# The gated adapter matrix of the second batch: from TensorE in batch 1's attention to ScalarE and GpSimd in batch 0's feed-forward half

## The chip, the cores and the metric

The kernel runs on one core of a Trainium2 chip, with every engine of that core: TensorE (PE; its weight loads, PEld, overlap its matmuls), VectorE (DVE), ScalarE (ACT), GpSimd (POOL) and SyncE (SP, which only issues DMAs). The metric is the device time of one execution in microseconds (us), as a median over runs. The kernel before takes 1123.19 us, the median of 3 runs from 1122.52 to 1124.55 us.

## The reference, cut to what matters

`x` is (2, 1024, 2048), `ctx` (2, 2048, 2048), the feed-forward weight `kernel` 2048 x 2048, all f32. There are 8 groups of 256 tokens (four to a batch), 16 adapters of rank 32, and a shared adapter.

```python
x = x + matmul(fake_quant(layernorm(x)), fake_quant(ctx))   # quantised cross attention
h = layernorm(x)
base   = matmul(h, kernel) + bias
A_eff  = einsum('bn,nri->bri', gate, lora_A)   # (8,16) x (16,32,2048): gated A of each group
B_eff  = einsum('bn,nor->bor', gate, lora_B)   # gated B
Ax     = einsum('bri,bti->btr', A_eff, h.reshape(8, 256, 2048))
delta  = einsum('bor,btr->bto', B_eff, Ax)
delta += einsum('or,btr->bto', lora_B_shared, einsum('ri,bti->btr', lora_A_shared, h))
x = x + base + delta
```

`A_eff` and `B_eff` are called the gated A and the gated B below. The change concerns only how the gated A of the second batch's four groups is made.

## The kernel before, in words

**Stages.** One loop runs over the two batches. Each turn has an attention stage and a feed-forward half (`ffn`). In the trace the product stage of the first feed-forward half lies at about 243 to 545 us; batch 1's attention starts inside its end and runs to about 790 us; the second feed-forward half follows.

**Attention.** The context comes in four blocks of 512 columns. Each block is loaded in eight tiles of 512 KB from `todo`, a list set out by hand at L155 to L164, which `load_next` (L170) works off in order on SP's queue, up to nine tiles ahead of use, each into a buffer of `lit` (ten buffers of 4 KB a partition). `quantise` (L310) rounds a tile to integers (ScalarE at L314 into one of the three `q2b` buffers, VectorE at L317 back out in bf16), `column_term` adds the zero-point term of the block, and `xattn_pair` (L350) multiplies one group's layernormed, quantised tokens by a block on TensorE (`pa`, L361) and adds it to `y`, the residual in SBUF. It also leaves layernorm sums in `st2`.

**The gated matrices.** `gated` (L376) makes one 128 x 512 piece of a gated matrix on TensorE: all 512 rows (16 adapters by 32) of a block of 512 columns stand in two `lit` tiles, loaded by four DMAs of 256 KB; four fp32 matmuls with `gmat`, the gates laid out as a matrix, sum over the adapters (L383); VectorE copies the PSUM result to a `q2b` buffer (L395). For A, `lora_a_step` (L398) then transposes the piece in four 128 x 128 parts on TensorE (L403) and VectorE copies them with four instructions to `acat` (L406), which holds A with the input dimension on the partitions: `acat[p, k, column, r]`, where the columns 0, 2, 3 and 5 belong to the four groups and 1 and 4 to the shared A. There are four such steps in a batch: two while block 2 is quantised (after its tiles 3 and 7) and two between the pairs of block 2. For B, `lora_b_step` (L411) stores the pieces to a DRAM tile `bd`.

**Between attention and feed-forward.** `prep_z` (L422) normalises a tile of 128 tokens with VectorE (L257 to L261 give its mean and deviation; `sd_z` at L261 is ScalarE's), transposes it on TensorE in packs of four (`ptz`, L432, two PSUM buffers, as `ps_m` has) and copies each pack out with ScalarE (L433). `group_z` (L435) stores each group's `z` to DRAM (`zs`) on ScalarE's DMA queue. `lora_ax` (L442) multiplies `acat` with z for two groups (`px`, L448), and ScalarE copies the result to `axT`.

**Feed-forward.** The 1024 x 2048 by 2048 x 2048 product is made by Strassen's scheme on two levels: 7 outer products (index `o`) of 7 inner products each (index `s`). `product` (L607) is one of these 49: 8 fp32 matmuls, which the trace records as 16 of 128 x 512, in PSUM chains named fu, fv and fw (L619), 6.87 us a product. `spread` adds a finished chain to the blocks of `y` with VectorE (L637). The operands are sums of blocks, built ahead by `Operands`: the left ones (names a and s) in `lit` buffers, loaded from `zs` and combined on GpSimd; the right ones (b and t) in `big` buffers, loaded from the weight and combined on VectorE; L559 is `block`, L568 is `comb`. The tables `BEGIN`, `BLOCKS`, `AHEAD`, `OWN` and `DROP` say behind which inner product each is loaded, combined and given back. `Delta.step` (L470) runs in inner products 1 and 4 of outer products 0 to 3: it loads a piece of the gated B and of the bias (`bp`, `bias`) on ScalarE's DMA queue, copies the bias into PSUM with ScalarE (L480, L483), multiplies by `axT` (`pl`, L491) and adds to `y` with VectorE (L502). There are eight such steps in a feed-forward half. The last outer product of batch 0 also starts batch 1's attention (`meanwhile`: block 0 is quantised and the first `prep_x` run).

**Order.** A scheduler places the instructions on each engine by their dependences and the program's order. `line` (L507) overrides it on VectorE alone: each of the feed-forward's VectorE additions is made to follow the one before it in the program. GpSimd's are placed by the scheduler.

**Layout that the change reaches.** `st1` and `st2` (L124, L125) are the layernorm sums of the attention input and output, each 128 x 8 x 4 x 6. `gate_b` is the gate on every partition, (8, 16); it is masked in place with `m_ad` at the program's start to make `gval`, from which `gmat` is filled for each batch. After the attention's block 2 in batch 0, the shared A is loaded to `acat` by SP (L750) and the shared B to `bd` (L753).

Of the kernel before, what the change touches and what calls it, by code (L numbers as in the profile page):

```python
# [10 lines left out]
F32 = mybir.dt.float32  # L11
# [4 lines left out]
ALU = mybir.AluOpType  # L16
# [4 lines left out]
P = 128  # L21
# [45 lines left out]
def tile_quant_xattn_then_lora_ffn(  # L67
# [32 lines left out]
    KQ = KT // 4  # L100
    GP = GPB * RC

    const = ctx.enter_context(tc.tile_pool(name="const", bufs=1))
# [4 lines left out]
    ps_m = ctx.enter_context(tc.tile_pool(name="ps_m", bufs=2, space=PSUM))  # L108
# [6 lines left out]
    q2b = Bufs([const.tile([P, 2, NB], I16, tag=f"q2b{i}", name=f"q2b{i}") for i in range(3)])  # L115

    acat = const.tile([P, KT, GPB // 2 * 3, R], F32, tag="acat", name="acat")
    own_col = [0, 2, 3, 5]
# [2 lines left out]
    bias_b = Bufs([const.tile([P, NB], F32, tag=f"bias{i}", name=f"bias{i}") for i in range(1)])  # L121
    axT = const.tile([P, GPB // 2, GT], F32, tag="axT", name="axT")
    gmat = const.tile([P, 2, GPB // 2, RC], F32, tag="gmat", name="gmat")
    st1 = const.tile([P, MT, NN, 6], F32, tag="st1", name="st1")  # L124
    st2 = const.tile([P, MT, NN, 6], F32, tag="st2", name="st2")  # L125
    r_s = const.tile([P, MT], F32, tag="r_s", name="r_s")

    zs = [
# [11 lines left out]
    def flat(t):  # L140
        return t.rearrange("p k n -> p (k n)")
# [14 lines left out]
    for b in range(B):  # L156
        for n in range(2):
            todo.extend((b, raw_src(b, n, r)) for r in range(KT // 2))
        for n in range(2, 4):
            for r in range(KT // 2):  # L160
                todo.append((b, raw_src(b, n, r)))
                if r in ((3, 7) if n == 2 else (5, 7)):
                    todo.extend((b, ad_src(la, 2 * (n - 2) + r // 6 if n == 3 else r // 4, h)) for h in range(2))
        for n in range(NN):  # L164
            todo.extend((b, ad_src(lb, n, h)) for h in range(2))
# [51 lines left out]
    ident = const.tile([P, P], F32, tag="ident", name="ident")  # L217
# [11 lines left out]
    for tag in ("acc0", "acc1", "delta"):  # L229
# [212 lines left out]
    def lora_ax(b, pr, zqs):  # L442
# [12 lines left out]
                )  # L455
        nc.scalar.copy(axT[:, pr, :], px)

    class Delta:


        def __init__(self, b):
            self.b = b


            self.banks = [ps_m.tile([P, NB], F32, tag="pm", name=f"pl_{b}_1{i}") for i in range(2)]
            for t in self.banks:
                nc.tensor.matmul(t, ones_h, ones_h[:, 0:1].to_broadcast([P, NB]), start=True, stop=True)
            self.units = deque((pr, n) for pr, n in ((0, 2), (0, 3), (0, 0), (0, 1), (1, 0), (1, 1), (1, 2), (1, 3)))
# [37 lines left out]

    def line(ins):  # L507

        if ins.ins.engine == mybir.EngineType.DVE:
            if line.last is not None:  # L510
                tc.add_manual_dep(
                    ins.ins,
                    line.last.name,
                    mybir.DependencyInfo(mybir.DependencyClass.NoSync, mybir.DependencyReason.DATA),
                    reason="line",
                )
            line.last = ins.ins

    line.last = None

    NO = len(OUTER)
    last_use = {}
# [4 lines left out]
    class Operands:  # L527
# [7 lines left out]
        def load(self, name):  # L535

            i, j = int(name[1]) - 1, int(name[2]) - 1
            a_terms, b_terms, _ = OUTER[self.o]
            got = []
            if name[0] == "a":  # L540
                for I, K, _ in a_terms:
                    t = lit.take()
                    nc.sync.dma_start(out=t, in_=zs[self.b][2 * I + i][2 * K + j])
                    got.append(t)
            else:
                for K, J, _ in b_terms:
                    t = big.take()
                    k0, n0 = (2 * K + i) * KQ * P, (2 * J + j) * NB
                    nc.sync.dma_start(out=t, in_=w[ds(k0, KQ * P), ds(n0, NB)].rearrange("(k p) n -> p k n", p=P))
                    got.append(t)  # L550
            self.wait[name] = got
# [91 lines left out]
    def ffn(b, ops, meanwhile):  # L643

        delta = Delta(b)
        for o in range(NO):
            nxt = Operands(b, o + 1) if o + 1 < NO else None
            chains = {}
            for s in range(len(INNER)):
                product(b, o, s, ops, chains)  # L650
                if s in OWN:
                    OWN[s](ops)
                if nxt and s in AHEAD:
                    AHEAD[s](nxt)
                spread(b, o, s, chains)
                if s in (1, 4):
                    delta.step()
                added = line.last
                if nxt:
                    for name in BLOCKS.get(s, ()):  # L660
                        nxt.block(name)
                for name in DROP.get(s, ()):
                    ops.drop(name)
                if nxt:
                    for name in BEGIN.get(s, ()):
                        nxt.load(name)
                with tc.issue_after(added):
                    meanwhile(o, s)
            ops = nxt
# [31 lines left out]
    for b in range(B):  # L701
# [30 lines left out]
        for g in range(2, GPB):  # L732
            for m in range(g * MG, (g + 1) * MG):
                with tc.issue_after(opened.ins):
                    prep_x(b, m, c1T, wk)
            for n in range(2):
                xattn_pair(b, n, g, c1T, c2[n])
                if g + 1 == GPB:
                    close_c2(n)
                    open_c2(n + 2)  # L740
                    bp.give(colt.pop(n))
                    if n == 0:
                        for r in range(NR):
                            quantise(c2[2], r)
                            if r % 4 == 3:
                                lora_a_step(b, r // 4)
                        column_term(b, 2, c2[2])
        if b == 0:
            for pr in range(GPB // 2):
                nc.sync.dma_start(out=acat[:, :, 3 * pr + 1, :], in_=a_sh)  # L750
            for bb in range(B):
                for g in range(GPB):
                    nc.sync.dma_start(out=bd[bb][g, 1 - g % 2], in_=b_sh)  # L753
        for g in range(GPB):
            xattn_pair(b, 2, g, c1T, c2[2])
            for r in {0: range(3), 1: range(3, 6), 2: range(6, 8), 3: ()}[g]:
                quantise(c2[3], r)
            if 1 <= g <= 2:
                lora_a_step(b, g + 1)
            if g == 2:  # L760
                column_term(b, 3, c2[3])
# [156 lines left out]
```

## Time and profile before

The profile is of one execution, which took 1122.67 us; the span from its first to its last instruction is 1120.9 us. It is 0.5 us under the median of the runs.

| | from the profile before |
|---|---|
| profiled execution, span | 1122.67 us, 1120.9 us |
| median of 3 runs (lowest to highest) | 1123.19 us (1122.52 to 1124.55) |
| matmuls of the feed-forward products, fu, fv and fw at L619 | 395.3 + 198.1 + 99.2 = 692.6 us, 593 ns each |
| attention matmuls, `pa` at L361 | 233.3 us, 381 ns each |
| GpSimd's 128 x 1024 operations, L559 and L568 | 99.8 + 160.3 us, 2497 and 2872 ns each |
| VectorE's 128 x 2048 operations, L559 and L568 | 102.2 + 161.5 us, 2554 and 2888 ns each |
| ScalarE's share of the span | 23% (261.6 us), most of it in the attention stages |
| DMA | 261.35 MB, 233 GB/s on average |
| of it adapter A (`lit<-in_lora_a_dram`) | 32 DMAs of 256 KB, SP's queue |

A row of the profile's groups names the line and engine, the operation, the tile written and the tiles read, partitions by elements, the count, then the busy time of the group in us with the mean of one in ns, and last the idle time of the engine before them and what ended most of it. The chain of waits is followed back from the last instruction, and gives 82% of its length to TensorE. The order of the rows of a timeline or a chain is that of time: start, length, engine, line, operation.

### The profile page before, as it was taken

The numbers are of one execution on the slowest core, as the hardware profiler recorded it, in microseconds if no ns is written. First come the engines' busy times: TensorE is split into PE (matmuls) and PEld (weight loads), VectorE is DVE, ScalarE is ACT, GpSimd is POOL, SyncE is SP. The second block draws the span as 40 slices with busy tenths as digits, with TensorE's granted clock in tenths as the row PEclk, the third lists the DMA queues.
The fourth block names the chain that finished last, engine by engine and source line by source line (L and its number), as shares of the span: only waits on it lengthen the run. The fifth ranks groups of instructions, "written<-read, shape, count | busy, mean of one in ns | idle before, by whom it ended". The sixth has DMA issues, their size and how long they took to land.

```text
span 1120.9 us, 10622 instructions
## 1 busy us (share of the span) xinstructions
PE 1066.2 (95%) x3898; PEld 493.9 (44%) x3930; DVE 745.5 (67%) x969; ACT 261.6 (23%) x358; POOL 260.7 (23%) x106
## 2 busy tenths in 40 slices
PE   1689999999999999999999999999999999999998
PEld 0344334554444444444444433455444444444443
DVE  4685547565697767668777654766568686865851
ACT  5875513220000000001375761232100000000000
POOL 0000000223353421534000000021534343253600
PEclk6799999999999999999999999999999999999999
DMA  8991946786789757499867095488768875749511
GB/s 307 393 248 36 281 127 233 265 319 234 246 283 374 281 175 261 153 328 322 286 187 226 1 280 151 180 301 313 253 225 293 302 260 175 260 145 322 208 38 56
DMA packets 120772, 261.35 MB, mean 233 GB/s; under 512 B 11920, under 2 KB 16144, under 8 KB 119568
## 3 DMA queue, kind: packets, MB, share of 16 engines
q1 hardware_dynamic: 99264, 218.65, 57.0%
q10 hardware_dynamic: 21456, 42.02, 11.0%
q8 instruction: 31, 0.51, 0.2%
q14 instruction: 21, 0.17, 0.0%
HBM read 224.99 MB, written 37.75 MB: 234 GB/s over the span
## 4 chain that ended last, share of the span: by engine, by line
PE 82%; DMA 7%; DVE 4%; ACT 4%; issue 1%; SPq 1%; ACTq 0%; DVEq 0%
PE fu L619 33%; PE fv L619 17%; PE pa L361 12%; PE fw L619 9%; DMA lit<-in_ctx_dram 4%; PE pl L491 3%; PE ptz L432 2%; DMA bd<-q2b 2%; DMA zs<-lit 1%; PE px L448 1%; PE pg_a L383 1%; DVE st L283 1%; PE pg_b L383 1%; ACT big L298 1%; ACT big L295 1%
## 5 line engine op out<-in xcount | busy, mean ns | idle before, releaser
L619 PE MATMUL fu<-big,lit 128*128 128x512 f32 x896 | 395.3, 593 | 0.0
L568 POOL TENSOR_TENSOR lit<-lit,lit 128x1024 f32<-128x1024 f32 x56 | 160.3, 2872 | 529.1 <-DMA zs<-lit 403.1
L619 PEld LDWEIGHTS fu<-big,lit 128*128 128x128 f32 x896 | 168.7, 190 | 206.2 <-issue 205.2
L361 PE MATMUL pa<-big,big 128*128 128x512 bf16 x992 | 233.3, 381 | 13.1 <-ACT pa L359 9.5
L619 PE MATMUL fv<-big,lit 128*128 128x512 f32 x448 | 198.1, 594 | 0.0
L559 POOL TENSOR_TENSOR lit<-lit,lit 128x1024 f32<-128x1024 f32 x40 | 99.8, 2497 | 293.6 <-DMA lit<-zs 261.9
L568 DVE TENSOR_TENSOR big<-big,big 128x2048 f32<-128x2048 f32 x56 | 161.5, 2888 | 5.7 <-PE ptz L432 5.1
L361 PEld LDWEIGHTS <-big 128*128 128x128 bf16 x1024 | 97.0, 98 | 144.5 <-issue 42.3
L637 DVE TENSOR_TENSOR y<-y,fu 128x1024 f32<-128x1024 f32 (+1 forms) x98 | 113.7, 1194 | 63.6 <-PE fu L619 63.3
L619 PEld LDWEIGHTS fv<-big,lit 128*128 128x128 f32 x448 | 84.3, 190 | 105.0 <-issue 104.7
L637 DVE TENSOR_TENSOR y<-y,fv 128x1024 f32<-128x1024 f32 x48 | 56.8, 1218 | 88.3 <-PE fv L619 88.3
L314 ACT ACTIVATE q2b<-lit,sc,inv 128x1024 int16<-128x1024 f32 x64 | 76.6, 1230 | 156.8 <-DMA lit<-in_ctx_dram 137.2
L559 DVE TENSOR_TENSOR big<-big,big 128x2048 f32<-128x2048 f32 x40 | 102.2, 2554 | 11.1 <-DMA big<-in_w_dram 11.1
L619 PE MATMUL fw<-big,lit 128*128 128x512 f32 x224 | 99.2, 592 | 0.0
L370 DVE SCALAR_TENSOR_TENSOR y<-pa,k_s,y 128x1024 f32<-128x1024 f32 x32 | 41.0, 1282 | 69.6 <-PE pa L361 69.6
L480 ACT COPY pl<-bias 128x1024 f32<-128x1024 f32 x16 | 16.3, 1018 | 293.9 <-DVE y L502 280.9
L359 ACT ACTIVATE pa<-bp,r_s 128x512 f32<-128x512 f32 x64 | 42.8, 683 | 105.4 <-PE pa L361 60.2
L619 PEld LDWEIGHTS fw<-big,lit 128*128 128x128 f32 x224 | 42.2, 190 | 51.8 <-issue 51.6
L637 DVE TENSOR_TENSOR y<-y,fw 128x1024 f32<-128x1024 f32 x24 | 28.4, 1217 | 50.5 <-PE fw L619 50.5
L303 PE MATMUL pt<-ident_h,big 128*128 128x128 bf16 x256 | 20.3, 231 | 29.7 <-ACT big L298 29.4
L283 DVE BATCH_NORM_STATS2 st<-y 128x6 f32<-128x512 f32 x64 | 42.0, 676 | 2.7 <-DMA y<-in_x_dram 2.7
L317 DVE TENSOR_SCALAR big<-q2b 128x1024 bf16<-128x1024 int16 x64 | 27.5, 439 | 22.6 <-ACT q2b L314 19.4
(82 smaller groups left out, 630.5 us busy)
## 6 DMA issues: line engine op xcount, KB each, us to landing
big<-in_w_dram SPq DMA_DIRECT2D x96, 1024.0 KB
lit<-zs SPq DMA_DIRECT2D x88, 512.0 KB
lit<-in_ctx_dram SPq DMA_DIRECT2D x64, 512.0 KB
out_dram<-y ACTq DMA_DIRECT2D x30, 512.0 KB
zs<-lit ACTq DMA_DIRECT2D x24, 512.0 KB
y<-in_x_dram SPq DMA_DIRECT2D x8, 1024.0 KB
lit<-in_lora_a_dram SPq DMA_DIRECT2D x32, 256.0 KB
lit<-in_lora_bt_dram SPq DMA_DIRECT2D x32, 256.0 KB
```

Of the source, the lines that this page charges most:

```text
L283: nc.vector.bn_stats(st1[:, m, n, :], ym[:, ds(n * NB, NB)])
L314: nc.scalar.activation(qi, t, AF.Relu, bias=z2, scale=inv2)
L317: nc.vector.tensor_scalar(c2[r // 4][:, ds(2 * (r % 4), 2), :], qi, QMAX, CENTRE, ALU.min, ALU.subtract)
L359: nc.scalar.activation(pa[:, j, :], colt[n], AF.Identity, bias=r_s[:, m : m + 1])
L361: nc.tensor.matmul(pa[:, j, :], c1T[g][:, k, ds(j * P, P)], c2[k // 8][:, k % 8, :], start=False, stop=(k == KT - 1), skip_group_check=True,)
L370: summed = nc.vector.scalar_tensor_tensor(yp, pa, s12, yp, ALU.mult, ALU.add)
L383: nc.tensor.matmul(ps[row : row + GP, :], gmat.rearrange("p i a r -> p (i a r)"), t[:, c, :], start=True, stop=True, skip_group_check=True,)
L491: nc.tensor.matmul(pl[j][i][:, half], axT[rows, pr, ds(j * P, P)], bt[rows, half], start=False, stop=True, skip_group_check=True,)
L559: line(eng.tensor_tensor(got[0], got[0], got[1], ALU.add if terms[1][2] > 0 else ALU.subtract))
L568: line(eng.tensor_tensor(out_t, at[p], at[q], op))
L619: nc.tensor.matmul(ps[:, m, :], at[:, k, ds(m * P, P)], bt[:, k, :], start=(opens and k == 0), stop=(ends and k == KQ - 1), skip_group_che ...
L637: line(nc.vector.tensor_tensor(yp, yp, chains[chain][:, js, :], ALU.add if sign > 0 else ALU.subtract))
```

## The change

**Batch 1's gated A is no longer made in its attention.** In `todo`, the adapter A tiles are listed for batch 0 only, and the four calls of `lora_a_step` are made for batch 0 only. The gated B stays as it was.

**A new class `Gates` makes it in the feed-forward half of batch 0.** An adapter is 32 x 2048 numbers; it is loaded as a tile of 128 partitions by 512 (partition = 4 r + quarter of the columns) by one DMA of 256 KB from GpSimd's queue. For each of the four groups ScalarE multiplies it by that group's gate for the adapter, a number per partition from `gate_b`, and GpSimd adds the product into `acat`'s columns of the group; the first adapter is multiplied straight into `acat`. So there are 64 ScalarE multiplies, 60 GpSimd additions and 16 loads. When an adapter is done, the next one's load is issued. `SLOTS` names the 16 places (outer and inner product) behind which one adapter each is done: outer products 0 to 5. In inner products 5 and 6 of outer product 5, `turn` brings each group's 128 x 512 sum into the layout of `acat`: ScalarE copies it to a buffer, TensorE transposes it in four parts (`pgt`, in the `ps_m` buffers), ScalarE copies the result to `acat`. Two groups are turned in each of the two places.

**Buffers.** The ring of four 128 x 512 buffers is made of the three `q2b` buffers, which the feed-forward half does not use until batch 1's context comes, and of `st`, a tile that now holds `st1` and `st2` as views.

**The gates.** `gate_b`, masked since the start of the program, is loaded again unmasked by one DMA on SP's queue, ahead of the shared A's loads.

**The order by hand.** `line` now fixes the order on each engine that it is given an instruction of. That is VectorE as before, and GpSimd: all its feed-forward additions, the new additions and the new loads follow the program's order. `spread`'s caller therefore takes VectorE's last instruction as `added`.

```diff
-    st1 = const.tile([P, MT, NN, 6], F32, tag="st1", name="st1")
-    st2 = const.tile([P, MT, NN, 6], F32, tag="st2", name="st2")
+    st = const.tile([P, NB], F32, tag="st", name="st")
+    st1, st2 = (st[:, ds(i * MT * NN * 6, MT * NN * 6)].rearrange("p (m n s) -> p m n s", n=NN, s=6) for i in range(2))
...
-                if r in ((3, 7) if n == 2 else (5, 7)):
+                if b == 0 and r in ((3, 7) if n == 2 else (5, 7)):
                     todo.extend((b, ad_src(la, 2 * (n - 2) + r // 6 if n == 3 else r // 4, h)) for h in range(2))
...
+    class Gates:
+        SLOTS = ((1, 3, 4), (1, 3), (1, 3), (1, 2, 3, 4), (1, 3, 4), (1, 3))
+
+        def __init__(self, b):
+            self.b = b
+            self.n = 0
+            self.turned = 0
+            self.bufs = [q2b.take() for _ in range(len(q2b.spare))]
+            self.ring = Bufs([st] + [flat(t).bitcast(F32) for t in self.bufs])
+            self.load()
+
+        def acc(self, g):
+            return acat[:, :, own_col[g], :]
+
+        def load(self):
+            self.t = self.ring.take()
+            src = lora_a[ds(self.n * R, R), :].rearrange("r (c i) -> (r c) i", i=NB)
+            line(nc.gpsimd.dma_start(out=self.t, in_=src))
+
+        def add(self):
+            t = self.t
+            for g in range(GPB):
+                gw = gate_b[:, self.b * GPB + g, self.n : self.n + 1]
+                if self.n == 0:
+                    nc.scalar.mul(self.acc(g), t.rearrange("p (k r) -> p k r", r=R), gw)
+                    continue
+                tmp = self.ring.take() if g + 1 < GPB else t
+                nc.scalar.mul(tmp, t, gw)
+                tv = tmp.rearrange("p (k r) -> p k r", r=R)
+                line(nc.gpsimd.tensor_tensor(self.acc(g), self.acc(g), tv, ALU.add))
+                if tmp is not t:
+                    self.ring.give(tmp)
+            self.ring.give(t)
+            self.n += 1
+            if self.n < NL:
+                self.load()
+
+        def turn(self, g):
+            t = self.ring.take()
+            nc.scalar.copy(t.rearrange("p (k r) -> p k r", r=R), self.acc(g))
+            pt = ps_m.tile([P, KQ, P], F32, tag="pm", name=f"pgt_{self.b}_{g}")
+            for k in range(KQ):
+                nc.tensor.transpose(pt[:, k, :], t[:, ds(k * P, P)], ident)
+            self.ring.give(t)
+            nc.scalar.copy(
+                acat[:, :, own_col[g], :].rearrange("p (c k) r -> p c k r", c=NN),
+                pt.rearrange("p k (r c) -> p c k r", c=NN),
+            )
+
+        def step(self, o, s):
+            if o < len(self.SLOTS) and s in self.SLOTS[o]:
+                self.add()
+            if self.n == NL and s > 4 and self.turned < GPB:
+                for _ in range(2):
+                    self.turn(self.turned)
+                    self.turned += 1
+                if self.turned == GPB:
+                    for t in self.bufs:
+                        q2b.give(t)
...
     def line(ins):
 
-        if ins.ins.engine == mybir.EngineType.DVE:
-            if line.last is not None:
-                tc.add_manual_dep(
-                    ins.ins,
-                    line.last.name,
...
+        eng = ins.ins.engine
+        if eng in line.last:
+            tc.add_manual_dep(
+                ins.ins,
+                line.last[eng].name,
...
+        line.last[eng] = ins.ins
...
         delta = Delta(b)
+        gates = Gates(b + 1) if b + 1 < B else None
...
                 if s in (1, 4):
                     delta.step()
-                added = line.last
+                added = line.last[mybir.EngineType.DVE]
+                if gates:
+                    gates.step(o, s)
...
-                            if r % 4 == 3:
+                            if b == 0 and r % 4 == 3:
                                 lora_a_step(b, r // 4)
...
         if b == 0:
+
+            nc.sync.dma_start(
+                out=gate_b.rearrange("p b n -> p (b n)"),
+                in_=gate.rearrange("b n -> (b n)").partition_broadcast(P),
+            )
             for pr in range(GPB // 2):
                 nc.sync.dma_start(out=acat[:, :, 3 * pr + 1, :], in_=a_sh)
...
-            if 1 <= g <= 2:
+            if b == 0 and 1 <= g <= 2:
                 lora_a_step(b, g + 1)
```

More of the change, by code (lines that the diff above doesn't have):

```diff
@@ L507, in line @@
     def line(ins):
-        if ins.ins.engine == mybir.EngineType.DVE:
-            if line.last is not None:
-                tc.add_manual_dep(
-                    ins.ins,
-                    line.last.name,
[L514 to L519, printed above, removed]
+        eng = ins.ins.engine
[3 more added lines that the diff above has]
+                line.last[eng].name,
+                mybir.DependencyInfo(mybir.DependencyClass.NoSync, mybir.DependencyReason.DATA),
+                reason="line",
+            )
+        line.last[eng] = ins.ins
+    line.last = {}
     NO = len(OUTER)
@@ L748, in tile_quant_xattn_then_lora_ffn @@
         if b == 0:
+            nc.sync.dma_start(
+                out=gate_b.rearrange("p b n -> p (b n)"),
+                in_=gate.rearrange("b n -> (b n)").partition_broadcast(P),
+            )
             for pr in range(GPB // 2):
```

## The prediction, as put on record before the changed kernel ran

> **What bounds the kernel now.** I read the busy shares, then the windows by stage, then the chain of waits in order of time, and last the timelines of the places that the change touches.
>
> ```profile
> PE 1066.2 (95%) x3898; PEld 493.9 (44%) x3930; DVE 745.5 (67%) x969; ACT 261.6 (23%) x358; POOL 260.7 (23%) x106
> POOL 0000000223353421534000000021534343253600
> ```
>
> TensorE is busy 95% of the span. GpSimd works only in the two feed-forward halves (FFN) and has room there. The windows of the first FFN, and of the stretch of batch 1's attention that holds its four `lora_a_step`s (columns: stretch, length, busy us of PE, PEld, DVE, ACT, POOL, clock, DMA share, GB/s):
>
> ```profile
> 243.00:545.00 302.00, 302.00 (x782) 136.78 (x782) 217.38 (x145) 19.33 (x25) 114.45 (x43) 1.00 0.77 270
> 640.70:689.80 49.10, 47.77 (x240) 19.24 (x244) 27.11 (x56) 20.91 (x22) 0.00 (x0) 1.00 0.72 204
> ```
>
> TensorE has no idle time at all in the first and 1.3 us in the second. So work taken off TensorE in the second counts nearly in full, and any wait that the change brings into the first counts in full too. The chain of waits prices the first two of the four steps (start, us, what):
>
> ```profile
> 640.81 0.98 PE pg_a L383 x2
> 641.78 2.48 PE pa L361 x11
> ...
> 645.34 0.99 PE pg_a L383 x6
> 646.33 2.26 PE pa L361 x10
> 648.60 0.44 PE pga L403 x4
> 649.03 0.99 PE pg_a L383 x8
> ...
> 652.59 0.45 PE pga L403 x4
> ...
> 653.54 9.23 DMA lit<-in_ctx_dram
> ```
>
> **The change part by part, batch 1's attention.** Removed from TensorE: 0.98+0.99+0.44 = 2.4 us for step 0, 0.99+0.45 = 1.4 us for step 1. Steps 2 and 3 come in two halves each like step 0 (between 668.8 and 686.6): 2 x 2.5 = 5.0 us, with the transposes nearer 0.5. Sum 8.8 us. VectorE loses 4 x (0.68 + 0.88) us at L395 and L406, and SP 16 issues of 256 KB, behind which the context tiles stood; nine tiles are loaded ahead, and now all eight of column block 2 are among them. What comes back: block 2 can now be quantised only as ScalarE goes, 1.23 us a tile (L314), and `column_term` follows the last tile. Walking the new order of TensorE from the second half of pair (0,3), I find about 1.1 us of waiting where 1.3 us stood. So 8.8 us net; bounds 5 us (if the 9.23 us context load in the chain still sets the pace) and 11 us (if VectorE's removed copies also free TensorE).
>
> **First FFN, TensorE.** `turn` adds 16 transposes in two packs of 8. A pack of 8 `ptz` transposes moves the next product from 225.38 to 226.25: 0.87 us, so +1.8 us.
>
> **First FFN, GpSimd.** 60 adds of 128x512 and 16 load issues. Nearest row: 2.35 us for 128x1024 (L559, L568). Bounds 1.18 us (half) and 2.35 us (if the 32-element runs of `acat` halve the rate). While VectorE has an add of two SBUF tiles under way, both rows stretch, VectorE's from 2.28 to 4.4 us:
>
> ```profile
> 310.55 4.24 DVE L559 TENSOR_TENSOR big<-big,big 128x2048 f32<-128x2048 f32 x1
> 314.82 4.33 DVE L568 TENSOR_TENSOR big<-big,big 128x2048 f32<-128x2048 f32 x1
> 319.07 2.34 DVE L637 TENSOR_TENSOR y<-y,fu 128x1024 f32<-128x1024 f32 x2
> ```
>
> Both look as if they waited for one operation of the other. Some 0.6 such waits of 2.28 us fall into four adds: 1.18 + 0.34 = 1.5; I take 1.6 us an add, 6.4 us an adapter. An issue on GpSimd: 0.33 us (the `bp` issue on ScalarE's queue) to 3.5 us (L750); I take 1.0. GpSimd then does 114 + 96 + 16 = 226 us of 302: it fits. VectorE's `spread` at 319.07 is done at 321.4, and the product that overwrites its PSUM tile starts at 324.1; one wait per operation is already paid there, so I charge 0.7 us for the whole FFN (0 to 4). The left operands are combined some 20 us ahead of use, and GpSimd's new fixed order (s4 before the next a11) and the adds eat 10 to 15 us of that: nothing, by this cover. Without it each late block would show on TensorE one for one. Loads: the same 4 MB, moved from SP's queue to GpSimd's, at a DMA share of 0.77: nothing.
>
> **First FFN, ScalarE.** 64 multiplies and 8 copies at 0.58 us (L483, 128x512): some 42 us into 302 us that hold 19. Not the work counts but the place in the queue. At the entry, four multiplies stand between `sd_z` at 220.35 and the copies of the last `ptz` tiles:
>
> ```profile
> 208.51 7.54 POOL L568 TENSOR_TENSOR lit<-lit,lit 128x1024 f32<-128x1024 f32 x3 [206.69 <-DMA zs<-lit]
> ...
> 220.35 0.30 ACT L261 ACTIVATE sd_z<-ve_z 128x1 f32<-128x1 f32 x2 [1.86 <-issue]
> 226.01 1.08 ACT L433 COPY big<-ptz 128x512 f32<-128x512 f32 x2 [5.36 <-PE ptz L432]
> ```
>
> The first load needs `st` free, which VectorE's last L257 gives at 216.9; behind it on GpSimd stands s3 (2.35 to 4.4 us), then the second load, at about 220.5 to 222. Landing after issue: 4.2 us (512 KB of `zs`, issued at 497.93, waited for until 502.1) to 6.9 us (`bias`, 241.70 to 248.62); I take 5. Two multiplies behind it end at 226.7 to 228.2, the first `ptz` copies wait for them, and TensorE has two `ptz` buffers: 0.7 to 2.2 us, and up to 4 with 6.9. I take 2.0. One more multiply (0.58 us) stands before the copy of `axT`, behind a product that was moved forward: 0.3 us. The `gate_b` reload on SP ahead of `acat`: one issue of 0.45 us, half of it on the path, 0.2.
>
> [...]
>
> ScalarE's queue also holds `Delta.step`'s copies behind the multiplies of the adapters before, and TensorE takes them here:
>
> ```profile
> 285.52 6.87 PE fw L619 x16
> 292.38 1.93 PE pl L491 x16
> 294.31 5.78 PE fu L619 x13
> ```
>
> Walk: adapter 1's adds 243.5 to 249.9, load issued to 250.9, landed 254.9; adapter 2's adds 255.5 to 261.9, load to 262.9; a22, s1, s2, a12, s3 to 275.9; adapter 3's adds to 282.3; adapter 4's load landed 287.3, four multiplies to 289.7, issue, first copy (1.02, L480) at 291.05. TensorE wants it at 292.38: 1.3 us to spare, so 0. The second such place, `pl` at 397.0, has some 4 us.
>
> Sum: -8.8 + 1.8 + 0.7 + 2.0 + 0.3 + 0.2 = -3.8 us. The profiled execution took 1122.67 us (span 1120.9, 1.8 around it): 1118.9. It lay 0.5 us under the median of the three runs, 1123.19, so the median should be about 1119.4.
>
> **The rivals.** *ScalarE's queue becomes the wait (slower).* One mechanism: the multiplies wait for loads that GpSimd issues only after the adds before, and the copies behind them are late at 226 and at 292. For: the margin at 292 is 1.3 us, and twelve adds and two landings lie in that walk, so adds over 1.7 us or landings over 5.6 us break it. Against: GpSimd has idle time that could take up part. With adds of 1.9 and landings of 6 us the same walk ends at 298.4 (6 us late) and the entry costs 3.2: -8.8+1.8+0.7+0.5+9.2 = +3.4, 1126.6 as a median. With 2.35 and 6.9 it is 13 us at 292, 4 at the entry, 4 at 397: 1138. It decides against the change from some 6 us of such waits on.
>
> *The attention stretch is paced by transfers, and the gain is 5.* For: the 9.23 us context load in the chain. Against: TensorE idles only 1.3 of 49.1 us there, and the loads ahead of the context tiles go away. -5+1.8+0.7+2.5 = 0: 1123.2, no change.
>
> *All goes well:* the entry's loads land in time: -8.8+1.8+0.3 = -6.7, 1116.5.
>
> That the change does not do what it says I leave out: the built instruction stream of batch 1 on TensorE holds no `pg_a`, and the 16 loads stand on GpSimd's queue.
>
> **How the numbers follow.** Forecast 0.38 (its own range 1117 to 1120.9), all goes well 0.08, transfers pace 0.17, ScalarE's queue 0.37. The first two give faster by over 0.2% (2.2 us, about what a measurement of this kernel can tell from no change): 0.46. The third is the same: 0.17. The last is slower: 0.37. The time is the forecast's, 1119.4. The range of 1113.5 to 1131 takes the lower bound of the gain's other end (11 us, no stall: 1114) and most of the slow rival.
>
> **What would show it.** Right: `pa` L361 unbroken by `pg_a` in batch 1 and that stretch some 8 to 9 us shorter; acat adds of 1.2 to 1.9 us on POOL; ACT's multiplies done before 228 at the entry and PE's `pl` without a wait. Wrong: idle time of PE in the first FFN released by ACT `ptz` or `pl`; a POOL add above 2 us; loads from POOL that take over 6 us; or an attention stretch that waits for `lit<-in_ctx_dram` instead.

## The result, and the profile after

The changed kernel is slower: 1130.54 us, the median of 11 runs (1126.52 to 1136.6), against 1123.18 us for the kernel before (11 runs, 1121.62 to 1125.87). The ratio is 1.0062, with a 95% interval of 1.0051 to 1.0073. The time lies inside the range on record, near its upper end; the forecast of 1119.4 us and its direction were wrong. The profiled execution took 1128.4 us with a span of 1126.6 us, 5.7 us more than the span before. It lies 2.1 us under the median of its runs, so what follows accounts for 5.7 of the 7.4 us between the medians.

The new lines L482 to L509 are those of `Gates`; L559, L568, L619, L637, L480 and L491 have become L626, L635, L686, L704, L547 and L558. First the busy shares and GpSimd's slices on the page of the changed kernel:

```profile
PE 1062.7 (94%) x3866; PEld 494.3 (44%) x3898; DVE 725.3 (64%) x949; ACT 307.9 (27%) x430; POOL 384.5 (34%) x182
POOL 0000000249765858687400000021534444071800
```

GpSimd works 124 us more, nearly all in the first feed-forward half, where its slices now reach 9 and mostly lie between 5 and 8. Next, the windows by stage of both kernels, cut where the work itself changes stage: from the first matmul of the first feed-forward half to its last, from there to the first of the second half, and to the last matmul. The columns are those of the windows in the prediction. Before:

```profile
191.77:585.85 394.08, 390.30 (x1222) 184.40 (x1223) 282.38 (x279) 62.56 (x90) 128.43 (x48) 1.00 0.77 267
585.85:728.80 142.95, 139.75 (x730) 60.83 (x741) 91.18 (x199) 66.63 (x88) 0.00 (x0) 1.00 0.54 168
728.80:1115.78 386.98, 384.98 (x1153) 181.17 (x1153) 254.22 (x201) 30.96 (x54) 130.97 (x48) 1.00 0.64 227
```

After:

```profile
192.08:601.30 409.22, 395.09 (x1239) 187.42 (x1240) 275.84 (x279) 108.86 (x162) 243.16 (x124) 0.99 0.75 267
601.30:735.45 134.15, 130.95 (x681) 58.55 (x693) 85.15 (x181) 66.51 (x87) 0.00 (x0) 1.00 0.47 149
735.45:1121.20 385.75, 384.14 (x1153) 180.57 (x1153) 246.45 (x200) 31.23 (x55) 140.04 (x48) 1.00 0.64 227
```

Batch 1's attention became 8.8 us shorter (142.95 to 134.15), as forecast: TensorE's busy time in it fell by 8.80 us, and its idle time stayed at 3.20 us. The first feed-forward half became 15.1 us longer (394.08 to 409.22), where the forecast had 4.8 us for everything that happens in it and at its entry. The second half is 1.2 us shorter. With 0.3 us at the start that makes 5.4 of the 5.7 us.

The waits of TensorE in that stretch of the changed kernel (waiting engine and line, what it waits for, us in total, times, longest):

```profile
PE pl L558 <- ACT pl L547: 5.3, 2, 3.4
PE fw L686 <- DVE big L626: 3.6, 2, 1.9
PE pt L303 <- ACT big L298: 3.5, 1, 3.5
```

Comparing the start of each of the 49 products in the two traces places the 15.1 us: 3.8 us at the `pl` matmuls of outer product 1, 5.1 us at those of outer product 3, 1.75 us at the two packs of `turn`, and 4.5 us in outer product 6 (1.8 us at its step 1, 2.7 us at step 5). The entry comes out even: the product that started at 248.9 us starts at 249.1, and 0.3 us of difference was there before. It is not free of waits, though. One of the two `fw` waits above, of 1.9 us, lies there (TensorE's timeline, then GpSimd's and VectorE's ahead of it):

```profile
221.04 5.42 PE L686 MATMUL fw<-big,lit 128*128 128x512 f32 x12 [1.92 <-DVE big L626]
215.75 0.69 POOL L482 DMA_DIRECT2D st<-in_lora_a_dram  x1 [1.16 <-DVE ve_z L259]
216.46 2.37 POOL L635 TENSOR_TENSOR lit<-lit,lit 128x1024 f32<-128x1024 f32 x1
217.09 3.89 DVE L626 TENSOR_TENSOR big<-big,big 128x2048 f32<-128x2048 f32 x1 [1.46 <-DMA big<-in_w_dram]
```

GpSimd's left operand stands behind the first load of `Gates`, and VectorE's right operand takes 3.89 us instead of 2.28 beside it. In its place two waits of 0.6 and 0.8 us for VectorE (`ptz`, L428), which the kernel before has at the entry, are gone.

**The first of the two `pl` waits, step by step.** GpSimd's timeline of the changed kernel (start, length; in brackets, where there is one, the idle time before and what ended it):

```profile
275.75 3.31 POOL L494 TENSOR_TENSOR acat<-acat,st 128x512 f32<-128x512 f32 x1
279.02 5.75 POOL L494 TENSOR_TENSOR acat<-acat,q2b 128x512 f32<-128x512 f32 x3
284.72 0.55 POOL L482 DMA_DIRECT2D st<-in_lora_a_dram  x1
```

ScalarE's timeline behind it:

```profile
290.83 1.95 ACT L492 ACTIVATE q2b<-st,gate_b 128x512 f32<-128x512 f32 x3 [21.98 <-DMA st<-in_lora_a_dram]
292.81 0.72 ACT L492 ACTIVATE st<-st,gate_b 128x512 f32<-128x512 f32 x1
292.87 0.33 ACTq L544 DMA_DIRECT2D bp<-bd  x1
293.44 1.00 ACT L547 COPY pl<-bias 128x1024 f32<-128x1024 f32 x1
```

And TensorE's:

```profile
294.50 2.96 PE L558 MATMUL pl<-bp,axT 64*128 64x256 f32 x16 [1.91 <-ACT pl L547]
297.39 2.83 PE L686 MATMUL fu<-big,lit 128*128 128x512 f32 x4
```

ScalarE stood idle for 22 us in front of a load that GpSimd could issue only at 284.72, when it had added the adapter before; the copies of `Delta.step` stood behind the four multiplies. TensorE waits 1.91 us, and then is slow for a while: `pl` takes 2.96 us instead of 2.00, and four product matmuls take 2.83 us where four of the kernel before take 1.88. The stretches of 3.41 us before and after the change of clock tell why (the granted clock is the third column from the end; the last row lies behind the second wait):

```profile
292.30:295.72 3.42, 1.51 (x12) 1.13 (x13) 2.35 (x2) 3.14 (x5) 3.03 (x2) 1.00 0.40 131
295.72:299.13 3.41, 3.41 (x10) 1.85 (x8) 3.19 (x5) 0.00 (x0) 3.41 (x3) 0.50 0.65 184
404.94:408.36 3.42, 3.42 (x15) 2.25 (x14) 1.78 (x3) 0.47 (x1) 3.42 (x4) 0.50 0.28 103
```

After each of the two waits the clock is at 0.50 for 3.41 us, which costs TensorE 1.7 us more: 1.91 + 1.7 of the 3.8 us, 3.43 + 1.7 of the 5.1 us. The second wait has the same shape; there GpSimd's four additions before the load took 13.1 us (its timeline):

```profile
381.99 3.31 POOL L494 TENSOR_TENSOR acat<-acat,st 128x512 f32<-128x512 f32 x1
385.26 9.92 POOL L494 TENSOR_TENSOR acat<-acat,q2b 128x512 f32<-128x512 f32 x3
395.12 0.55 POOL L482 DMA_DIRECT2D st<-in_lora_a_dram  x1
```

One such addition is 1.27 us at the median and 3.37 us at most (the tile view's row: count, minimum, median and maximum in ns):

```profile
L494 POOL TENSOR_TENSOR acat<-acat,q2b x45: 1243/1270/3372, 244.8 to 519.1; 128x512 f32<-128x512 f32 x45
```

All four between 381.99 and 395.12 took 3.3 us, each beside one of VectorE's additions of two SBUF tiles (four of them started between 381.59 and 390.70). An instruction that is stretched so is called held below.

**The last outer product.** SyncE's timeline of the changed kernel there:

```profile
514.94 8.09 SPq L610 DMA_DIRECT2D lit<-zs  x2
523.14 0.38 SPq L616 DMA_DIRECT2D big<-in_w_dram  x1
...
540.03 0.37 SPq L176 DMA_DIRECT2D lit<-in_ctx_dram  x1
540.50 0.41 SPq L616 DMA_DIRECT2D big<-in_w_dram  x1
```

Before, the same first context load was issued at 514.19 and that weight load at 518.03. TensorE is 10 us behind here, yet these loads are 26 and 22 us later: they stand on SP's queue behind loads that wait for GpSimd to give a `lit` buffer back, and GpSimd is busy with the last adapter (513.3 to 520.3). The context tiles (L314) stand ahead of the first `prep_x` on ScalarE: its `sd_a` starts at 569.83 us, right behind two of them, instead of 553.55, and `pt` at step 5 waits for its copies (L298). At step 1 the late weight load is not alone: VectorE's two additions ahead of the operand that TensorE waits for took 3.02 and 4.33 us instead of 2.28, beside GpSimd's operands, and the two causes of the 1.8 us were not separated.

### The profile page after: what moved, and what is told of

Read it like the earlier page. It is cut to its first block, busy times and chain, and to the rows that moved or that the text cites. A ratio compares the mean times of both kernels' runs of the same rounds, so it can differ in the third digit from the quotient of the medians.

```text
span 1126.6 us, 10687 instructions
## 1 busy us (share of the span) xinstructions
PE 1062.7 (94%) x3866; PEld 494.3 (44%) x3898; DVE 725.3 (64%) x949; ACT 307.9 (27%) x430; POOL 384.5 (34%) x182
## 5 line engine op out<-in xcount | busy, mean ns | idle before, releaser
L686 PE MATMUL fu<-big,lit 128*128 128x512 f32 x896 | 396.8, 595 | 0.0
L635 POOL TENSOR_TENSOR lit<-lit,lit 128x1024 f32<-128x1024 f32 x56 | 149.6, 2675 | 651.9 <-PE pa L361 398.5
L686 PEld LDWEIGHTS fu<-big,lit 128*128 128x128 f32 x896 | 169.1, 191 | 206.4 <-issue 204.1
L686 PE MATMUL fv<-big,lit 128*128 128x512 f32 x448 | 198.1, 594 | 0.0
L704 DVE TENSOR_TENSOR y<-y,fu 128x1024 f32<-128x1024 f32 (+1 forms) x98 | 113.6, 1193 | 70.8 <-PE fu L686 70.2
L635 DVE TENSOR_TENSOR big<-big,big 128x2048 f32<-128x2048 f32 x56 | 153.1, 2736 | 5.8 <-PE ptz L432 5.2
L626 POOL TENSOR_TENSOR lit<-lit,lit 128x1024 f32<-128x1024 f32 x40 | 120.1, 3010 | 41.2 <-DMA lit<-zs 37.1
L686 PEld LDWEIGHTS fv<-big,lit 128*128 128x128 f32 x448 | 84.3, 190 | 105.0 <-issue 104.8
L704 DVE TENSOR_TENSOR y<-y,fv 128x1024 f32<-128x1024 f32 x48 | 56.8, 1217 | 89.3 <-PE fv L686 89.3
L626 DVE TENSOR_TENSOR big<-big,big 128x2048 f32<-128x2048 f32 x40 | 99.1, 2477 | 18.9 <-DMA big<-in_w_dram 18.9
L686 PE MATMUL fw<-big,lit 128*128 128x512 f32 x224 | 99.4, 593 | 3.6 <-DVE big L626 3.6
L494 POOL TENSOR_TENSOR acat<-acat,q2b 128x512 f32<-128x512 f32 x45 | 84.8, 1905 | 10.1 <-ACT q2b L492 10.1
L314 ACT ACTIVATE q2b<-lit,sc,inv 128x1024 int16<-128x1024 f32 x64 | 76.4, 1230 | 38.6 <-DMA lit<-in_ctx_dram 25.1
L686 PEld LDWEIGHTS fw<-big,lit 128*128 128x128 f32 x224 | 42.0, 190 | 55.4 <-issue 52.2
L704 DVE TENSOR_TENSOR y<-y,fw 128x1024 f32<-128x1024 f32 x24 | 28.4, 1216 | 55.6 <-PE fw L686 55.6
L547 ACT COPY pl<-bias 128x1024 f32<-128x1024 f32 x16 | 16.2, 1015 | 167.9 <-DVE y L569 150.0
L492 ACT ACTIVATE q2b<-q2b,gate_b 128x512 f32<-128x512 f32 x36 | 25.0, 715 | 75.4 <-DMA q2b<-in_lora_a_dram 55.9
```

What stands on the lines that cost most here:

```text
L314: nc.scalar.activation(qi, t, AF.Relu, bias=z2, scale=inv2)
L492: nc.scalar.mul(tmp, t, gw)
L494: line(nc.gpsimd.tensor_tensor(self.acc(g), self.acc(g), tv, ALU.add))
L547: nc.scalar.copy(own, bb.unsqueeze(1).to_broadcast([P, 2, NB]))
L626: line(eng.tensor_tensor(got[0], got[0], got[1], ALU.add if terms[1][2] > 0 else ALU.subtract))
L635: line(eng.tensor_tensor(out_t, at[p], at[q], op))
```

## The experiments

Each was timed against the kernel before on the same chip.

**ScalarE's order by hand (e1).** `Delta.step`'s three copies and `Gates`' multiplies are put through `line`, which keeps the program's order on ScalarE.

```diff
-                nc.scalar.mul(tmp, t, gw)
+                line(nc.scalar.mul(tmp, t, gw))
...
-                nc.scalar.copy(self.banks[i], bb)
+                line(nc.scalar.copy(self.banks[i], bb))
...
```

> Delta.step's copies and the multiplies of Gates follow the program's order on ScalarE, so no multiply of a later adapter stands ahead of a Delta copy. Theory Q (the order of ScalarE's queue cost 8.9 us: 3.8 us at pl of outer product 1, step 1, and 5.1 us at that of outer product 3, each wait with one window of half clock of 3.4 us behind it): both waits go, 1130.5 - 8.9 = 1121.6 us. Rival G (GpSimd has too little time for the additions, the queue only shows it): the wait comes back as left operands that TensorE waits for, 1128 to 1132 us.

Measured: 1123.73 us (12 runs, 1121.3 to 1127.03), ratio 1.0002 (0.9991 to 1.0012): 6.8 us less than the changed kernel. TensorE's waits in that half of this kernel no longer have a `pl` row:

```profile
PE pt L303 <- ACT big L298: 3.0, 1, 3.0
PE fw L686 <- issue: 1.3, 1, 1.3
PE fu L686 <- DVE y L704: 0.5, 1, 0.5
```

The same copies now run at 267.29 us, 26 us sooner. Theory Q holds: an order on ScalarE, and not a lack of time, made the 8.9 us. The time did not fall by as much: there are 2.1 us of new waits in outer product 4 (the fw and fu rows; the fw wait ends 0.1 us after a right operand of VectorE, two of whose additions just before took 3.8 and 4.3 us beside GpSimd's), and outer product 6 keeps 3.8 us (the pt row, with one stretch of half clock behind it), which this edit does not touch.

**The last slot moved to outer product 1 (e2).**

```diff
-        SLOTS = ((1, 3, 4), (1, 3), (1, 3), (1, 2, 3, 4), (1, 3, 4), (1, 3))
+        SLOTS = ((1, 3, 4), (1, 3, 4), (1, 3), (1, 2, 3, 4), (1, 3, 4), (1,))
```

> Order on ScalarE as in the changed kernel; the last adapter's slot (outer product 5, step 3) moves to outer product 1, step 4. Theory L (the additions of the last two adapters delay GpSimd's last left operands, their release of lit, and so the loads behind it on SP's queue: 4.5 us in the last outer product): 1130.5 - 4.5 = 1126 us, or 1128 if only one of the two waits goes. [...]

Measured: 1133.11 us (6 runs), ratio 1.0089 (1.0069 to 1.0109), not faster than the changed kernel. The expectation missed the time, since it left out what the move does to the `pl` waits (TensorE's waits in this kernel):

```profile
PE pl L558 <- ACT pl L547: 10.4, 2, 7.7
```

In outer product 6, which the theory was about, the 4.5 us fell to 1.3 us.

**Both edits (e3).**

> Both edits. Q and L together: 1130.5 - 8.9 - 4.5 = 1117.1 us, faster than both kernels. G: over 1123 us, with TensorE waiting for left operands in outer products 1 to 5.

Measured: 1121.46 us (12 runs, 1118.14 to 1128.32), ratio 0.9986 (0.9967 to 1.0004). The time lies between the 1117.1 us expected of Q and L and G's 1123. The profiled execution is the fastest of the 12, 3.3 us under their median. In it neither a `pl` wait nor a half clock between the start and the last microsecond is left (the granted clock over its span is 0.998); what remains, apart from the entry, is `turn`, 0.6 us in outer product 6, and waits for operands at outer products 2 (1.1 us) and 4 (3.3 us).

**`Gates` left out (e4).** `gates = None` in `ffn`; batch 1 is computed with batch 0's gated A.

> Leaves out the loads, multiplies, additions and turns of Gates; batch 1 is computed with batch 0's gated A. What is left is the removal of lora_a_step from batch 1 and GpSimd's fixed order. If all 15.1 us lost in the first feed-forward half come from Gates: 1130.5 - 15.1 = 1115.4 us, with no idle time of TensorE there. If GpSimd's fixed order has a part in them: 1117 to 1121 us, with waits for left operands left.

Measured: 1114.45 us (6 runs, 1113.83 to 1117.28), ratio 0.9923 (0.9911 to 0.9935). The first feed-forward half takes 393.90 us, as before the change (394.08). So the removal is worth some 9 us, and `Gates` costs the half all of its 15 us, as a net sum. Within the half this kernel is not like the one before: its entry is 1.5 us shorter, and TensorE still waits in outer product 6, where the kernel before has 0.8 us:

```profile
PE pt L303 <- ACT big L298: 2.0, 1, 2.0
```

The first context load of that stretch is issued at 522.18 us instead of 514.19, with no adapter on GpSimd; what is left on GpSimd is its fixed order. So 1.2 of the 4.5 us in outer product 6 belong to the order, and against this kernel the entry of the changed one costs 1.4 us.

**One slot moved, from e3 (e5).** `SLOTS = ((1, 3, 4), (1, 3, 4), (1, 3, 4), (1, 3, 4), (1, 3, 4), (1,))`.

> e3_both with one slot moved: three adapters in each of outer products 0 to 4 and one in 5 (e3 has four in a row in outer product 3). Theory L: the waits left in e3 at outer product 4, step 1 (2.7 us) and 2, step 1 (1.1 us) come from additions crowded ahead of left operands and from VectorE's additions that they collide with; the first goes: 1121.5 - 2.7 = 1118.8 us. Rival: the collisions only move with the slots, 1121 to 1123 us.

Measured: 1124.7 us (12 runs), ratio 1.0003 (0.9989 to 1.0016). The wait of 2.7 us at outer product 4 is gone, and one of 2.4 us stands at outer product 3. The rival was right that the holds move with the slots, though its 1121 to 1123 us were passed. This is how they look on VectorE, whose addition of 2.28 us alone takes 3.5 and 4.3 us before that wait (its timeline):

```profile
380.52 3.47 DVE L626 TENSOR_TENSOR big<-big,big 128x2048 f32<-128x2048 f32 x1
384.02 4.32 DVE L635 TENSOR_TENSOR big<-big,big 128x2048 f32<-128x2048 f32 x1
```

**Multiply and add on VectorE (e6).** ScalarE has no multiplies and GpSimd no additions; loads go three adapters ahead.

```diff
...
-                nc.scalar.mul(tmp, t, gw)
...
-                line(nc.gpsimd.tensor_tensor(self.acc(g), self.acc(g), tv, ALU.add))
+                line(nc.vector.scalar_tensor_tensor(self.acc(g), tv, gw, self.acc(g), ALU.mult, ALU.add))
```

> No multiplies on ScalarE and no additions on GpSimd: VectorE does multiply and add in one instruction per group and adapter (64 of 128x512, estimated 0.65 us from L370's 1.28 us for 128x1024, 42 us into the 302 us of the stage, which hold 201), and the loads are issued three adapters ahead. Theories Q and L: with ScalarE's queue free of multiplies and GpSimd free of additions only turn's 1.8 us is left over e4's 1114.5 us: 1116.3 us. Rival V: VectorE's spreads come late and hold PSUM, up to 1 us in each of 16 slots: 1120 to 1132 us.

Measured: 1137.43 us (6 runs), ratio 1.012 (1.0099 to 1.0141). Rival V, and worse than its price. One such instruction is 0.74 us alone, but these too read SBUF twice, and beside GpSimd's operand additions, all that GpSimd adds in this kernel, they take up to 2.9 us (minimum, median, maximum of the smaller group):

```profile
L499 DVE SCALAR_TENSOR_TENSOR acat<-st,gate_b,acat x12: 745/2088/2901, 314.1 to 483.7; 128x512 f32<-128x512 f32 x12
```

TensorE then waits for VectorE's spreads and right operands, in a profile with five stretches of 3.41 us at half clock in this half (granted clock over its span 0.99).

**GpSimd's fixed order alone**, on the kernel before (e8).

> The kernel before with the changed order by hand alone: GpSimd's additions in both feed-forward halves follow the program's order; nothing of Gates, lora_a_step stays. If the order is what shortens the second half by some 1 us: 1122.2 us and no wait in the first half. If the fixed order itself makes left operands late (a part of the 15.1 us): over 1125 us.

Measured: 1125.96 us (12 runs, 1122.79 to 1128.18), ratio 1.0021 (1.0011 to 1.0032). Neither expectation fits: it costs 2.7 us, but its profile shows no wait for a left operand. Its first feed-forward half is 2.2 us longer: the entry is 1.3 us shorter, as in e4, and one wait of 2.5 us for ScalarE in the last outer product, where the kernel before has 0.8 us, costs 3.4 us with one stretch of half clock behind it. Its second half is not shorter (386.9 us).

**GpSimd left to the scheduler**, once in e3 (e9) and once in the changed kernel itself (e11).

```diff
+        if eng == mybir.EngineType.Pool:
+            return
         if eng in line.last:
```

> e3_both with GpSimd's instructions left to the scheduler, as in the kernel before (order by hand on VectorE and ScalarE only). e8 showed GpSimd's fixed order alone to cost 2.7 us. If that price is paid in e3 too: 1121.5 - 2.7 = 1118.8 us. If GpSimd's additions, free to move, are put ahead of left operands by the scheduler: 1123 to 1130 us.

> The changed kernel with one part undone: GpSimd is left to the scheduler. If the fixed order has a part in the loss as in e8: 1130.5 - 2.7 = 1127.8 us, the waits at pl unchanged in place. If the fixed order protects the left operands from the additions: 1131 to 1140 us.

Measured: 1132.75 us (6 runs), ratio 1.0074 (1.0049 to 1.0099), and 1170.14 us (4 runs), ratio 1.0414 (1.0401 to 1.0428). In the second, one `pl` waits 23.2 us (its TensorE waits):

```profile
PE pl L558 <- ACT pl L547: 23.2, 1, 23.2
PE fw L688 <- DVE big L628: 17.7, 2, 17.4
```

Both are above what was expected of them. With `Gates` in place, the fixed order saves 40 us in the changed kernel and 11 us in e3. It is a needed part of the change, though alone, on the kernel before, it cost 2.7 us.

**Two groups in one addition (e10).** `st` and the `q2b` buffers become one tile of four, so that GpSimd adds groups 0 and 2, then 1 and 3, in one instruction of 128x1024 each; ScalarE's order and the slots as in e3.

```diff
...
-                line(nc.gpsimd.tensor_tensor(self.acc(g), self.acc(g), tv, ALU.add))
+                    a2 = acat[:, :, 2 * h : 2 * h + 4 : 3, :]
+                    tv = ring[:, ds(2 * h, 2), :].rearrange("p g (k r) -> p k g r", r=R)
+                    line(nc.gpsimd.tensor_tensor(a2, a2, tv, ALU.add))
...
```

> e3_both with two groups in one GpSimd addition (32 of 128x1024 less two, instead of 60 of 128x512). Theory C (each addition can be held once by an addition of VectorE that reads two SBUF tiles, and four in a row were): half as many holds, some 1 us less at each of 15 adapters on GpSimd, and the waits of 2.7 us in e3 shrink: 1118.5 to 1120 us. Rival: it is VectorE that loses (its 2.28 us additions are held by GpSimd's, now 2.35 us long instead of 1.27): 1122 to 1125 us.

Measured: 1118.32 us (6 runs, 1116.46 to 1121.79), ratio 0.9954 (0.994 to 0.9968): faster than both kernels, and 3.1 us less than e3. GpSimd's addition groups in e3 (busy us, mean ns of one):

```profile
L494 POOL TENSOR_TENSOR acat<-acat,q2b 128x512 f32<-128x512 f32 x45 | 89.6, 2012 | 12.2 <-ACT q2b L492 12.2
L494 POOL TENSOR_TENSOR acat<-acat,st 128x512 f32<-128x512 f32 x15 | 25.1, 1676 | 5.9 <-ACT st L492 5.9
```

And in this kernel:

```profile
L497 POOL TENSOR_TENSOR acat<-acat,ring 128x1024 f32<-128x1024 f32 x30 | 97.4, 3268 | 14.4 <-ACT ring L493 14.4
```

The additions take 97.4 us instead of 114.7, 1.2 us less for each of 15 adapters. TensorE waits for no `pl` and for no operand by more than 0.5 us in outer products 1 to 5, and outer product 6 has the 1.2 us that e4 has without `Gates`.

**The pairs without the other two edits (e12), and with ScalarE's order only (e13).**

> The changed kernel with one part altered: two groups in one GpSimd addition, ScalarE's order and the slots as in the change. Theory Q (the order on ScalarE is what makes the pl copies late): the waits at pl stay, shortened by what GpSimd gains before them (about 1 us an adapter): 1126 to 1130 us. Theory C alone (the holds on GpSimd are the whole cause, ScalarE's order harmless once they are fewer): 1118 to 1120 us.

> e12 with ScalarE's order by hand (e10_pairs with the changed kernel's slots). If the early slots are needed for the last outer product: 1118.3 + 3 = 1121 us with a wait in outer product 6; if the pairs give GpSimd enough room there: 1118 to 1119 us.

Measured: 1131.14 us (6 runs), ratio 1.0073 (1.0057 to 1.009), and 1121.88 us (11 runs), ratio 0.9993 (0.9982 to 1.0004). The first is just above theory Q's 1126 to 1130 us; it keeps a `pl` wait of 5.0 us at 292 us and is no faster than the changed kernel: fewer holds alone do not help while the copies stand behind multiplies that wait for loads. The second loses 5.5 us at step 5 of outer product 6, where e10 loses 1.2: the early slot is needed besides.

## Why the prediction was wrong, by its own steps

| step of the sum | forecast, us | measured, us |
|---|---|---|
| batch 1's attention | -8.8 | -8.8 |
| `turn` on TensorE | +1.8 | +1.75 |
| entry, with the multiply before `axT` | +2.3 | 0 against the kernel before, +1.4 against e4 |
| `gate_b` reload | +0.2 | not told apart (the half starts 0.3 us later) |
| holds, as far as they reach TensorE by `spread` | +0.7 | 0 |
| first `pl` (292 us) | 0 | +3.8 |
| second `pl` (397 us) | 0 | +5.1 |
| left operands and what follows from them, outer product 6 | 0 | +4.5 |
| second feed-forward half | not in it | -1.2 |

**What was right.** The gain on TensorE and the price of `turn` came out to a tenth. The rival *ScalarE's queue becomes the wait* named the mechanism and both places inside the feed-forward half; e1 shows it by undoing the order alone. It put a wait for ScalarE at the entry too, where there was none, and gave the whole 1126.6 us. Its own walk was summed too high: redone with additions of 1.9 us and landings of 6 us, and the other steps as they stand, it ends at 296.7, not 298.4 (4.3 us late), and with 2.35 and 6.9 us at 303.8 (11.4 us late, not 13).

**The step that failed** is the walk that gave `pl` "1.3 us to spare, so 0" and the second place "some 4 us". Set against the trace: adapter 2's load was issued by 252.3 instead of 250.9 us, GpSimd reached adapter 3's additions at 275.75 instead of 275.9, and up to there the walk was right. Then those four additions took 9.0 us instead of 6.4, since two were held, the load landed 6.0 us after its issue began instead of 5, and the first copy ended at 294.44, not 291.05. Holds were priced at 0.6 in four additions, which is too few, and their scatter was not priced at all: over the whole half, 108 us for 60 additions of 1.26 us are some 32 us of holds, 16 of 2.05 us, or 1.1 in four; at the second `pl` it was four in four. A spare of 1.3 us behind twelve such additions is no cover.

**A cost that no step had** is the half clock behind a wait: 1.7 us twice, 3.4 of the 8.9 us.

**Holds reach TensorE by the right operands, not by `spread`.** The term of 0.7 us followed VectorE's holds to `spread` alone. There TensorE waited for nothing, but it waited 1.9 us at the entry for a right operand that GpSimd had held, and the wait of 2.4 us in e5 has the same cause; those at the start of outer product 4 in e1 and e3 look like it.

**"The left operands: nothing, by this cover"** held as far as TensorE waits for no left operand, and failed in the last outer product by another path. The walk followed GpSimd's operands to TensorE, but not the `lit` buffers that they give back, nor the weight and context loads behind them on SP's queue. e2 and e10 against e13 show that the last adapter's slot makes most of it (4.5 to 1.3 us; 5.5 at step 5 alone to 1.2). The 1.2 us that stay are there in e4 without any adapter: the fixed order delays the same loads.

**The entry** was charged 2.3 us for a wait behind ScalarE that did not come. The second load landed at 224.6 us and the two multiplies behind it ended at 226.0, 0.7 us ahead of the walk; the `ptz` copies stood behind them, but TensorE had the product of step 1 to do in that time, and ScalarE then waited for it (0.96 us, to 226.93). That the entry comes out even is luck: the load on GpSimd makes a wait of 1.9 us through VectorE there, and the fixed order takes away 1.3 us (e8) to 1.5 us (e4) of others. Each kernel with `Gates` and the fixed order has that wait at step 1 (1.7 to 2.1 us, 3.3 in e6), and neither the kernel before nor e4 or e8 has one over 0.3 us.

GpSimd's load instruction is 0.55 us at the median and 0.69 at most, where the forecast took 1.0. Counted from the end of that instruction, six of the 16 loads landed in 2.2 to 2.4 us; the others took up to 6.2 us, in a stretch where the DMA engines are 0.75 busy. What made these slower was not shown.

**Open.** The second half's 1.2 us: GpSimd's order is not its cause (e8). The profiles of e1 to e6, e10, e12 and e13, whose second half is the same, give 385.2 to 386.7 us, so it may be no more than differs from one execution to the next. Runs of the changed kernel spread over 10 us, those before over 4; waits that turn on landings and on the phase of a clock window would do that, but this was not shown: only one execution of each kernel was profiled.

## What to carry to other kernels

Work on idle engines was not free here, because instructions that the busy engine needed stood behind it: ScalarE's copies behind its multiplies cost 8.9 us, and an order by hand took both waits away (e1). So write the order by hand on every engine that serves the critical one, before reckoning the time. A walk whose spare time is smaller than the scatter of its terms (here 1.3 us against holds of 2 us each) counts as a wait, not as cover. For two engines that hold each other, fewer and longer instructions were better here: half as many additions, with the order and one slot mended, turned +0.6% into -0.5%. The order and the slot gave about 0.8 points of that (e3), the longer additions the other 0.3 (e3 to e10).

## What the runs showed of the hardware

**A wait of 1.9 us can cost 3.6 us**, 1.91 us and 1.7 at half clock behind it. In the traces of the two kernels the granted clock changes only at times that lie whole multiples of 3.413 us apart: the two falls in the changed kernel, at 295.72 and 404.94 us, are 32 of them apart, and each lasts just one. Cut into these windows from 195 us to the last matmul, the two traces have three in which TensorE was idle for over half, all in the changed kernel: 85% (2.91 us, in the second `pl` wait) and 56% (the wait of 1.91 us), each followed by half clock, and 57% (1.93 us), followed by full clock. The kernel before fell to half clock at 41.44 us, behind a window idle for 65% (2.20 us). The place of a wait among the windows seems to matter: the 3.48 us wait at 573.7 us of the changed kernel was split by a boundary into the 57% and 45%, and cost no clock. What told the 56% from the 57% these traces do not say.

**GpSimd and VectorE held each other for whole instructions**, where both added two SBUF tiles: in the changed kernel 16 of the 60 additions of `Gates` took 3.30 to 3.37 us instead of 1.27 (1.27 + 2.04, beside VectorE's 2.28 us), each with such an addition of VectorE beside it, and VectorE's 2.28 us became up to 4.37. One hold lasted for several instructions of the other engine. In e3 an addition of VectorE took 9.56 us and ended 2.2 us, about its own length, after GpSimd had done five in a row (VectorE's row, then GpSimd's):

```profile
454.21 9.56 DVE L635 TENSOR_TENSOR big<-big,big 128x2048 f32<-128x2048 f32 x1
454.39 2.37 POOL L626 TENSOR_TENSOR lit<-lit,lit 128x1024 f32<-128x1024 f32 x1
456.71 2.48 POOL L494 TENSOR_TENSOR acat<-acat,q2b 128x512 f32<-128x512 f32 x2
459.15 1.25 POOL L494 TENSOR_TENSOR acat<-acat,st 128x512 f32<-128x512 f32 x1
460.37 1.25 POOL L494 TENSOR_TENSOR acat<-acat,q2b 128x512 f32<-128x512 f32 x1
```

The runs of 32 elements in `acat` cost nothing that shows: 2.37 us at the median for 1024 elements (e10), as for `lit` in the changed kernel (2.36 and 2.37).
